# Fewer history tiles fetched by address on SyncE, and two TensorE layers replaced by ScalarE operations, in an attention kernel for recommendation

## The chip, the cores and the metric

The kernel runs on one core of a Trainium2 chip. The time is device microseconds of one execution; the number before is the median of three runs.

The engines are written as the profile writes them: PE is TensorE, DVE is VectorE, ACT is ScalarE, POOL is GpSimd and SP is SyncE. POOL, ACT and SP can also issue DMA transfers.

## What is computed

A batch of 16384 users has 200 history positions each. For each position the item's row of 64 floats is looked up in a table of 100000 rows, weighed by a small attention network, and summed:

```python
h = i_emb[hist]                                  # (200, 16384, 64)
itb = jnp.broadcast_to(it[None], h.shape)
feat = jnp.concatenate([h, itb, h - itb, h * itb], axis=-1)
a = dice(feat @ au_W1 + au_b1, au_alpha, axis=1)  # 36 units
w = a @ au_W2 + au_b2
cur = jnp.sum(w * jax.lax.stop_gradient(h), axis=0)
z = jnp.concatenate([u, it, c, cur], axis=-1)
z = dice(z @ W1 + b1, alpha1, axis=0)
z = dice(z @ W2 + b2, alpha2, axis=0)
return z @ W3 + b3
```

with

```python
def dice(x, alpha, axis):
    mean = jnp.mean(x, axis=axis, keepdims=True)
    var = jnp.var(x, axis=axis, keepdims=True)
    p = jax.nn.sigmoid((x - mean) * jax.lax.rsqrt(var + EPS))
    return x * (p + alpha * (1.0 - p))
```

The statistics of `dice` in the attention run over the whole batch, so the gate of position l can be made only when all of position l has gone through the first layer.

## The kernel before

A *tile* is 128 table rows of 64 floats. A history position l has 128 tiles, worked on in ND = 8 *chunks* of TD = 16 tiles. A step `step(k)` stands for one chunk, k = 8 l + c. Positions 0 to 179 run in a hardware loop of two passes of LPB = 90 positions, and the last 20 stand outside of it, before the head. The order of instructions on each engine is the order in which the program is written.

**How rows arrive.** Two ways are used.

- `fetch(k)` has POOL gather tiles: one indirect DMA for each tile of 128 rows (line 124), into `rows[k % 5]`, with indices from `idx`.
- The last tile of the chunks in SIDES = (3, 5, 7), three tiles of each l, comes *by address*. The 384 indices of l are loaded (`load_addresses`, line 137), scaled to byte offsets on DVE at step c = 4 of the position before (`scale_addresses`, line 141), read into registers, and each row is fetched by one small DMA of its own (`ask`, line 294) into one of BUFS = 6 buffers `side`. SPLIT = 0.5 gives half of each step's share, 24 rows, to SP and half to ACT. The wait for a tile's 128 rows and the copy into `rows` are DVE's (`place_tile`, line 392).

So NC = 125 tiles of each l are gathered by POOL and 3 come by address.

**What a step does.** In the order of the program, step k:

1. POOL: the gathers of chunk k.
2. ACT: `hidden(k-2)` moves the first layer's sums out of PSUM, `px` to `xs` (line 377). At the end of a position DVE makes its mean and variance (`moments`).
3. SP and ACT: the rows by address of this step. ACT's part stands partly before and partly behind the gate.
4. ACT: `gate(k-9)` makes the sigmoid from `xs` into PSUM `pg` (line 366).
5. DVE: `place(k-1)` copies the side tile if there is one; `turn(k-1)` transposes `rows` into `hT` by four instructions (line 149).
6. PE, still in `turn`: a layer with the identity matrix `unit` copies `hT` into PSUM `ph`; two layers with `blk_h` and `blk_i` add to `px`.
7. DVE: the statistics of chunk k-2 (line 382); `product(k-1)` multiplies `ph` by the item's rows into `hm` (line 412), and PE adds the layer with `blk_m` to `px`.
8. DVE: `weights(k-9)` multiplies gate and `xs` into `y` (line 369). PE adds `blk_x` times `xs` and `blk_p` times `y` in `wb`: `blk_x` carries alpha times the second layer's weights, `blk_p` carries one minus alpha times them, so their sum is the second attention layer behind `dice`.
9. DVE: `weigh(k-9)` multiplies `wb` by `hT` (line 373) and adds it to `curT` (line 374).

All layers have one helper, line 154; in the trace one layer of a chunk is four matmul instructions of 128x512.

The user rows are gathered in the same way in the last eight steps, with the tiles of chunks 3 and 5 by address; the item rows are gathered in the set-up, with no tile by address.

Of the kernel before, what the change touches and what calls it, by code (L numbers as in the profile page):

```python
# [11 lines left out]
AF = mybir.ActivationFunctionType  # L12
ALU = mybir.AluOpType
PSUM = bass.MemoryType.PSUM

P = 128
# [7 lines left out]
LAG = 9  # L24
XR = 8
IDX = 3
SIDES = (3, 5, 7)
BUFS = 6
LOAD = 28
SPLIT = 0.5  # L30
ROW = 4 * D
U8 = mybir.dt.uint8

# [2 lines left out]
def din_kernel(  # L36
# [24 lines left out]
    nc = tc.nc  # L61
# [8 lines left out]
    ZB = Z1 - ZA  # L70
    NS = len(SIDES)
    serial = iter(range(10**6))
# [8 lines left out]
    def make(name, *shape, dt=F32):  # L81
        return const.tile(list(shape), dt, name=name)

    def col(v):
        return v.rearrange("(p o) -> p o", o=1)

    def quarter(e, g, n=S):
        return slice((2 * e + g) * S, (2 * e + g) * S + n)


    def column(c, n):
        if c in SIDES and n == TD - 1:
            return NC + SIDES.index(c)
        return c * TD + n - sum(s < c for s in SIDES)

# [4 lines left out]
    ph = psum.tile([P, CD], F32, name="ph")  # L100
    pg = psum.tile([P, CD], F32, name="pg")
    wb = psum.tile([P, CD], F32, name="wb")

    rows = [make(f"rows{i}", P, TD, D) for i in range(ROWS)]
    hT = [make(f"hT{i}", P, CD) for i in range(LAG)]
    xs = [make(f"xs{i}", P, CD) for i in range(XR)]
# [3 lines left out]
    y = make("y", P, CD)  # L110
# [35 lines left out]
    def transpose(dst, of, n=slice(0, TD)):  # L146
        for i in range(2):
            for e in range(2):
                nc.vector.transpose(by_tile(dst[ts(e, D)], i)[:, n], of[ts(i, D), n, ts(e, S)])  # L149

    def layer(dst, pairs, first=True, last=True):
        for i in range(2):
            for j, (lhsT, rhs) in enumerate(pairs):
                nc.tensor.matmul(  # L154
                    dst[:, ts(i, CH)], lhsT, rhs[:, ts(i, CH)],
                    start=(first and j == 0), stop=(last and j == len(pairs) - 1),
                    skip_group_check=not (first and last),
                )
# [24 lines left out]
    blk_i = make("blk_i", P, P)  # L183
    blk_m = make("blk_m", P, P)
    blk_p = make("blk_p", P, P)
    blk_x = make("blk_x", P, P)
    unit = make("unit", P, P)
    au_w = make("au_w", P, 4, A)
    au_bias = make("au_bias", P, 1)
    au_al = make("au_al", P, 1)  # L190
    au_1al = make("au_1al", P, 1)
# [4 lines left out]
    def attention_weights():  # L196
        for t in (blk_h, blk_i, blk_m, blk_p, au_bias, au_al, au_w2):
            nc.vector.memset(t, 0.0)
        nc.sync.dma_start(au_bias2, au_b2.partition_broadcast(P))
        for e in range(2):  # L200
            w = au_W1.rearrange("(g d) a -> d g a", d=D)[e * S : (e + 1) * S]
            for g in range(2):
                r = quarter(e, g)
                nc.sync.dma_start(au_w[r], w)
                for q, (a0, n) in enumerate(halves):
                    c, a = quarter(q, g, n), slice(a0, a0 + n)
                    nc.vector.tensor_add(blk_h[r, c], au_w[r, 0, a], au_w[r, 2, a])
                    nc.vector.tensor_sub(blk_i[r, c], au_w[r, 1, a], au_w[r, 2, a])
                    nc.vector.tensor_copy(blk_m[r, c], au_w[r, 3, a])
                    nc.vector.memset(blk_p[r, quarter(q, g)], 1.0)  # L210
        for g in range(2):
            for q, (a0, n) in enumerate(halves):
                r, a = quarter(q, g, n), slice(a0, a0 + n)
                nc.sync.dma_start(au_bias[r], col(au_b1)[a])
                nc.sync.dma_start(au_al[r], col(au_alpha)[a])
                nc.sync.dma_start(au_w2[r], au_W2[a])
        nc.vector.tensor_scalar(au_1al, au_al, -1.0, 1.0, ALU.mult, ALU.add)
        nc.vector.tensor_mul(au_1al, au_1al, au_w2)
        nc.vector.tensor_mul(au_al, au_al, au_w2)
        nc.vector.tensor_scalar_mul(blk_x, blk_p, au_al)  # L220
        nc.vector.tensor_scalar_mul(blk_p, blk_p, au_1al)
        nc.vector.tensor_copy(unit, lanes)
        nc.vector.tensor_single_scalar(unit, unit, float(P), ALU.is_equal)


    w1a = make("w1a", P, 4, P)
# [13 lines left out]
    lanes, lane = (ucT[i][:, :P].bitcast(I32) for i in range(2))  # L240
# [40 lines left out]
    def tiles_by_address(l):  # L281

        return l * NS, range(NS)
# [20 lines left out]
    def shares(n, s, split):  # L304

        many = round(n * split)
        runs = []
        for r0, end in ((s * n, s * n + many), (s * n + many, (s + 1) * n)):
            loads = -(-(end - r0) // LOAD)
            at = [r0 + (end - r0) * i // loads for i in range(loads + 1)]  # L310
            runs.append(list(zip(at, at[1:])))
        return runs

    def ask(queue, runs, first, tiles, at, table):
        engine = queues[queue][0]
        flat = table.rearrange("v d -> (v d)").bitcast(U8)

        def place_of(r):
            return tiles[r // P] * P + r % P

        for r0, end in runs:
            while r0 < end:
                many = end - r0
                while place_of(r0 + many - 1) != place_of(r0) + many - 1:
                    many -= 1
                _, loaded = nc.values_load_multi_w_load_instructions(
                    at[:, place_of(r0) : place_of(r0) + many],
                    engines=(engine,), min_val=0, max_val=ROW * (table.shape[0] - 1),
                    skip_runtime_bounds_check_because="scale_addresses holds the address to the table",
                )  # L330
                for r, a in enumerate(loaded, r0):
                    m, p = first + r // P, r % P
                    key = keys.setdefault(m, f"rows{next(serial)}")
                    dma = row_by_address(
                        queue,
                        side[m % BUFS].bitcast(U8)[p : p + 1],
                        flat[ds(a, ROW)].rearrange("(o d) -> o d", o=1),
                    ).then_inc(landed[m % BUFS], 16)
                    tc.no_tile_sem_insts.add(dma.ins.name)
                    tc.add_to_no_dep_group(key, dma.ins)  # L340
                r0 += many

    def ask_hist(k, queue, some):
        l, s = divmod(k, ND)
        first, tiles = tiles_by_address(l)
        runs = shares(len(tiles) * P // ND, s, SPLIT)[queue]
        ask(queue, runs[some], first, tiles, addr[l % 3], i_emb)
# [7 lines left out]
    def has_side(k):  # L355
        return k % ND in SIDES

# [6 lines left out]
    def gate(k):  # L364
        i = k // ND % 3
        nc.scalar.activation(pg, xs[k % XR], AF.Sigmoid, bias=shifts[i], scale=rstds[i])  # L366

    def weights(k):
        nc.vector.tensor_mul(y, pg, xs[k % XR])  # L369
        layer(wb, [(blk_x, xs[k % XR]), (blk_p, y)])  # L370

    def weigh(k):
        nc.vector.scalar_tensor_tensor(wb, wb, au_bias2, hT[k % LAG], ALU.add, ALU.mult)  # L373
# [10 lines left out]
    def place(k):  # L384
        if has_side(k):
            l, c = divmod(k, ND)
            first, tiles = tiles_by_address(l)
            place_tile(k, first + tiles.index(SIDES.index(c)))

    def place_tile(k, m):  # L390
        await_rows(m)
        nc.vector.tensor_copy(rows[k % ROWS][:, TD - 1], side[m % BUFS])  # L392
# [12 lines left out]

    def turn(k):
        transpose(hT[k % LAG], rows[k % ROWS])
        layer(ph, [(unit, hT[k % LAG])])
        layer(px, [(blk_h, hT[k % LAG]), (blk_i, itT[k % ND])], last=False)

    def product(k):
# [23 lines left out]
    def step(k, last=None, weighed=()):  # L435

        def has(j):
            return last is None or j <= last

        ends = (k - 2) % ND == ND - 1  # L440
        if has(k):
            fetch(k)
        if has(k - 2):
            hidden(k - 2)
            if ends:
                measure(k - 2)
                moments((k - 2) // ND)
        if has(k):
            ask_hist(k, 0, slice(None))
            ask_hist(k, 1, slice(0, 1))  # L450
        if k - LAG not in weighed:
            gate(k - LAG)
        if has(k):
            ask_hist(k, 1, slice(1, None))
        if has(k - 1):
            place(k - 1)
            turn(k - 1)
        if has(k - 2) and not ends:
            measure(k - 2)
        if has(k - 1):  # L460
            product(k - 1)
        if k - LAG not in weighed:
            weights(k - LAG)
            weigh(k - LAG)
# [336 lines left out]
```

## Time and profile before

| | us |
|---|---|
| median of three runs | 31699.99 |
| the three runs | 31647.45, 31703.36, 31699.99 |
| the profiled execution | 31646.96 |
| its span, first to last instruction | 31645.1 |
| PE busy | 20823.3 (66%) |
| DVE busy | 15548.7 (49%) |
| ACT busy | 3817.4 (12%) |
| POOL busy | 23853.6 (75%) |

The mean granted TensorE clock was 0.806. The rows of the profile that follow below are read so: a group of instructions is given by line, engine, operation, output and inputs, shapes and count; then its busy time in us and the mean of one in ns; then the idle time of the engine just before them, with what ended most of it. "issue" marks idle time in which the engine waited for nothing that the profile shows.

### The profile page before, as it was taken

How to read it: one execution, taken by the hardware profiler on the slowest of the kernel's cores; microseconds unless marked ns; L12 is line 12 of the kernel's file. 1: busy time of each engine (PE TensorE's matmuls, PEld its weight loads, DVE VectorE, ACT ScalarE, POOL GpSimd, SP SyncE). 2: the span in 40 equal slices, each digit the busy share in tenths (PEclk: the TensorE clock that was granted, in tenths of full speed). 3: DMA queues.
4: the chain of work that ended last, by engine and by line, in shares of the span. 5: the costliest groups of instructions: out<-in, count | busy, mean ns of one | idle time of the engine just before them, and what ended most of it. 6: DMA issues, size and time to landing. Idle time of an engine off the chain costs nothing.

```text
span 31645.1 us, 223489 instructions
## 1 busy us (share of the span) xinstructions
PE 20823.3 (66%) x39536; PEld 8584.9 (27%) x39536; DVE 15548.7 (49%) x21275; ACT 3817.4 (12%) x3322; POOL 23853.6 (75%) x25259
## 2 busy tenths in 40 slices
PE   6666666666666666666666666666666666666666
PEld 2222222222222222222222222222222222222222
DVE  5444444444444444444444444444444444444445
ACT  1111111111111111111111111111111111111111
POOL 7777777777777777777777777777777777777776
PEclk8888788887888888888788888887878788887888
DMA  2111111111111111111111111111111111111111
GB/s 44 28 28 28 28 28 28 28 28 28 28 28 28 28 28 28 28 28 28 28 28 28 28 28 28 28 28 28 28 28 28 28 28 28 28 28 28 28 28 30
DMA packets 1008142, 894.16 MB, mean 28 GB/s; under 512 B 597358, under 2 KB 597559, under 8 KB 1006695
## 3 DMA queue, kind: packets, MB, share of 16 engines
q0 software_dynamic: 808128, 829.14, 15.0%
q1 hardware_dynamic: 114362, 27.92, 0.4%
q10 hardware_dynamic: 84205, 22.70, 0.3%
q14 instruction: 1136, 9.31, 0.1%
q8 instruction: 311, 5.10, 0.1%
HBM read 873.48 MB, written 4.39 MB: 28 GB/s over the span
## 4 chain that ended last, share of the span: by engine, by line
POOL 30%; issue 11%; PE 6%; DMA 5%; DVE 2%; DVEq 0%; ACT 0%; POOLq 0%; ACTq 0%
POOL rows L124 30%; DMA rows<-in_L_rec_i_emb,idx 5%; PE px L154 3%; PE ph L154 2%; PE wb L154 2%; DVE hT L149 1%; DVE wb L373 1%; DVE curT L374 0%; DVE st L382 0%; DVEq L149 0%; DVE mv L418 0%; DVE rows L392 0%; DVE addrs L141 0%; POOLq L124 0%; PE pg L154 0%
## 5 line engine op out<-in xcount | busy, mean ns | idle before, releaser
L124 POOL DMA_INDIRECT rows<-in_L_rec_i_emb,idx x25000 | 23591.6, 944 | 7633.1 <-issue 7166.6
L154 PE MATMUL ph<-hT,unit 128*128 128x512 f32 x6404 | 5969.6, 1088 | 10697.5 <-DVE hT L149 10697.5
L373 DVE SCALAR_TENSOR_TENSOR wb<-wb,au_bias,hT 128x1024 f32<-128x1024 f32 x1609 | 2079.7, 1293 | 10748.4 <-PE wb L154 10748.4
L149 DVE STREAM_TRANSPOSE hT<-rows 64x512 f32<-64x512 f32 x6404 | 4518.5, 706 | 2971.8 <-DMA rows<-in_L_rec_i_emb,idx 2529.3
L154 PEld LDWEIGHTS ph<-hT,unit 128*128 128x128 f32 x6404 | 1796.1, 311 | 13756.3 <-DVE hT L149 13561.4
L154 PE MATMUL px<-hT,blk_h 128*128 128x512 f32 x6404 | 4065.3, 723 | 0.0
L377 ACT ACTIVATE xs<-px,au_bias 128x1024 f32<-128x1024 f32 x1602 | 1784.1, 1114 | 14492.6 <-PE wb L154 14492.5
L366 ACT ACTIVATE pg<-xs,sh,rs 128x1024 f32<-128x1024 f32 x1609 | 1943.3, 1208 | 12967.9 <-issue 10092.6
L154 PE MATMUL px<-itT,blk_i 128*128 128x512 f32 x6404 | 3382.0, 610 | 0.0
L154 PE MATMUL wb<-y,blk_p 128*128 128x512 f32 x6436 | 3291.1, 593 | 11.3 <-DVE y L369 11.3
L154 PE MATMUL wb<-xs,blk_x 128*128 128x512 f32 x6436 | 3289.2, 593 | 2.6 <-DVE curT L374 2.6
L154 PE MATMUL px<-hm,blk_m 128*128 128x512 f32 x6408 | 3011.3, 592 | 0.0
L412 DVE TENSOR_TENSOR hm<-ph,itT 128x1024 f32<-128x1024 f32 x1601 | 1960.4, 1224 | 1934.9 <-PE ph L154 1934.9
L154 PEld LDWEIGHTS px<-hT,blk_h 128*128 128x128 f32 x6404 | 1627.8, 254 | 2406.1 <-issue 2304.8
L382 DVE BATCH_NORM_STATS2 st<-xs 128x6 f32<-128x512 f32 x3204 | 2058.4, 684 | 44.5 <-ACT pg L366 0.3
L369 DVE TENSOR_TENSOR y<-pg,xs 128x1024 f32<-128x1024 f32 x1609 | 1955.7, 1215 | 85.0 <-ACT pg L366 82.9
L374 DVE TENSOR_TENSOR curT<-wb,curT 128x1024 f32<-128x1024 f32 x1609 | 1969.8, 1224 | 54.8
L154 PEld LDWEIGHTS px<-itT,blk_i 128*128 128x128 f32 x6404 | 1404.8, 219 | 2000.0 <-issue 2000.0
L154 PEld LDWEIGHTS wb<-y,blk_p 128*128 128x128 f32 x6436 | 1224.5, 190 | 1551.8 <-issue 1537.2
L154 PEld LDWEIGHTS wb<-xs,blk_x 128*128 128x128 f32 x6436 | 1224.3, 190 | 1541.4 <-issue 1538.0
L154 PEld LDWEIGHTS px<-hm,blk_m 128*128 128x128 f32 x6408 | 1219.0, 190 | 1531.4 <-issue 1524.2
L124 POOL DMA_INDIRECT rows<-in_L_rec_i_emb,ids x125 | 139.7, 1118 | 39.6 <-issue 37.2
(180 smaller groups left out, 1779.3 us busy)
## 6 DMA issues: line engine op xcount, KB each, us to landing
side<-in_L_rec_i_emb SPq DMA_DIRECT2D x38400, 0.2 KB
side<-in_L_rec_i_emb ACTq DMA_DIRECT2D x38400, 0.2 KB
rows<-in_L_rec_i_emb,idx POOLq DMA_INDIRECT x25000, 2.5
idx<-in_r_hist SPq DMA_DIRECT2D x200, 62.5 KB
hT<-cs ACTq DMA_DIRECT2D x16, 500.0 KB
ucT<-catT SPq DMA_DIRECT2D x8, 512.0 KB
side<-in_L_rec_u_emb SPq DMA_DIRECT2D x256, 0.2 KB
addrs<-in_r_hist SPq DMA_DIRECT2D x200, 1.5 KB
```

The costliest lines, as they stand in the source:

```text
L124: nc.gpsimd.indirect_dma_start(out=dst[:, n, :], out_offset=None, in_=table, in_offset=bass.IndirectOffsetOnAxis(ap=ids, axis=0),)
L149: nc.vector.transpose(by_tile(dst[ts(e, D)], i)[:, n], of[ts(i, D), n, ts(e, S)])
L154: nc.tensor.matmul(dst[:, ts(i, CH)], lhsT, rhs[:, ts(i, CH)], start=(first and j == 0), stop=(last and j == len(pairs) - 1), skip_group_c ...
L366: nc.scalar.activation(pg, xs[k % XR], AF.Sigmoid, bias=shifts[i], scale=rstds[i])
L369: nc.vector.tensor_mul(y, pg, xs[k % XR])
L373: nc.vector.scalar_tensor_tensor(wb, wb, au_bias2, hT[k % LAG], ALU.add, ALU.mult)
L374: nc.vector.tensor_add(curT[k % ND], wb, curT[k % ND])
L377: nc.scalar.activation(xs[k % XR], px, AF.Identity, bias=au_bias)
L382: nc.vector.bn_stats(stats[l % 3][:, 2 * c + i, :], xs[k % XR][:, ts(i, CH)])
L412: nc.vector.tensor_mul(hm, ph, itT[k % ND])
```

## The change

Three constants and four places in the code change.

- SIDES goes from (3, 5, 7) to (7,): one tile of each l, 128 rows, comes by address, and 127 are gathered by POOL. NC, the number of columns of `idx` and the number of addresses follow from it. The user pass, which takes the tiles of chunks 3 and 5 by address where they are in SIDES, then has none by address.
- SPLIT goes from 0.5 to 1.0: all rows by address are issued by SP, 16 in each step, and ACT issues none in the steps.
- In `turn`, a copy on ACT from `hT` to `ph` takes the place of the layer with `unit`.
- In `gate`, a second activation on ACT makes `au_1al` times the sigmoid plus `au_al`, in place in PSUM; `weights` then multiplies by `xs` on DVE as before, and PE has the one layer `blk_p` (of ones) instead of `blk_x` and `blk_p`. The matrices `unit` and `blk_x` and their making fall away.

```diff
-SIDES = (3, 5, 7)
+SIDES = (7,)
...
-SPLIT = 0.5
+SPLIT = 1.0
...
-        nc.vector.tensor_scalar_mul(blk_x, blk_p, au_al)
-        nc.vector.tensor_scalar_mul(blk_p, blk_p, au_1al)
-        nc.vector.tensor_copy(unit, lanes)
-        nc.vector.tensor_single_scalar(unit, unit, float(P), ALU.is_equal)
...
-            loads = -(-(end - r0) // LOAD)
+            loads = max(1, -(-(end - r0) // LOAD))
...
     def gate(k):
         i = k // ND % 3
         nc.scalar.activation(pg, xs[k % XR], AF.Sigmoid, bias=shifts[i], scale=rstds[i])
+        nc.scalar.activation(pg, pg, AF.Identity, bias=au_al, scale=au_1al)

     def weights(k):
         nc.vector.tensor_mul(y, pg, xs[k % XR])
-        layer(wb, [(blk_x, xs[k % XR]), (blk_p, y)])
+        layer(wb, [(blk_p, y)])
...
     def turn(k):
         transpose(hT[k % LAG], rows[k % ROWS])
-        layer(ph, [(unit, hT[k % LAG])])
+        nc.scalar.copy(ph, hT[k % LAG])
         layer(px, [(blk_h, hT[k % LAG]), (blk_i, itT[k % ND])], last=False)
```

More of the change, by code (lines that the diff above doesn't have):

```diff
@@ L185, in din_kernel @@
     blk_p = make("blk_p", P, P)
-    blk_x = make("blk_x", P, P)
-    unit = make("unit", P, P)
     au_w = make("au_w", P, 4, A)
```

## The prediction

> **What bounds the kernel now.** I read the page first: the busy shares, then the chain that ended last.
>
> ```profile
> span 31645.1 us, 223489 instructions
> PE 20823.3 (66%) x39536; PEld 8584.9 (27%) x39536; DVE 15548.7 (49%) x21275; ACT 3817.4 (12%) x3322; POOL 23853.6 (75%) x25259
> POOL 30%; issue 11%; PE 6%; DMA 5%; DVE 2%; DVEq 0%; ACT 0%; POOLq 0%; ACTq 0%
> ```
>
> No engine is busy all the time, and the chain accounts for 54% of the span only: it names a suspect, POOL and the "issue" gaps between its instructions, and proves nothing. So I read next all that POOL does, the gathers into `rows`, with what its idle time waited for (columns of the first rows: shortest/median/longest in ns, then the first and last start in us; of the others: us in total, times).
>
> ```profile
> L124 POOL DMA_INDIRECT rows<-in_L_rec_i_emb,idx x25000: 940/944/1120, 184.6 to 31408.0; - x199
> L124 POOL DMA_INDIRECT rows<-in_L_rec_i_emb,ids x125: 940/953/11142, 2.9 to 182.1; - x125
> L124 POOL DMA_INDIRECT rows<-in_L_rec_u_emb,ids x125: 940/944/961, 31409.2 to 31564.1; - x125
> L124 POOL DMA_INDIRECT rows<-in_L_rec_u_emb,side_ids x1: 944/944/944, 31565.3 to 31565.3; - x1
> ...
>   issue: 7241.2, 23739
>   DMA rows<-in_L_rec_i_emb,idx: 336.0, 1102
>   DVE rows L392: 55.2, 157
> ```
>
> The 25000 history gathers start evenly over 31223.4 us, so one starts every 31223.4 / 24999 = 1.249 us: 0.944 us of work and a gap. The gap put down to "issue" is 7241.2 / 23739 = 0.305 us, and the one put down to another gather 336.0 / 1102 = 0.305 us: the same, so neither is a wait for data. POOL therefore issues gather after gather without a stall that counts, from 184.6 us to 31565.3 us; 79.8 us of head follow, and before it stand 184.6 us. The number of gathers sets the time.
>
> Next, whether anything else is near that pace. The waits of DVE, which works on each chunk of 16 tiles (1600 chunks):
>
> ```profile
> DVE wb L373 <- PE wb L154: 10748.4, 1609, 7.5
> DVE hT L149 <- DMA rows<-in_L_rec_i_emb,idx: 2529.3, 1181, 5.0
> DVE hm L412 <- PE ph L154: 1934.9, 1601, 2.4
> ```
>
> The second row is the important one: DVE runs out of gathered rows, 2529.3 / 1600 = 1.6 us in each chunk. The consumers wait for POOL; they follow it closely, but they follow.
>
> **The change part by part.** *The gathers.* With SIDES = (7,) each history position l has 127 tiles of 128 by gather instead of 125. Over 200 positions that is 400 more instructions on POOL, and in the user pass at the end, where tiles 3 and 5 came by address, 2 more (128 for 126); the item pass keeps its 128. Each costs the pace above, on the engine that sets the end: 402 x 1.249 = 502.1 us. The gather of 128 rows is the same instruction on the same tables, so the price is not in doubt by more than the pace may shift; see the rivals.
>
> *The rows by address.* They go from 384 to 128 per l, all on SP:
>
> ```profile
> side<-in_L_rec_i_emb SPq DMA_DIRECT2D x38400, 0.2 KB
> side<-in_L_rec_i_emb ACTq DMA_DIRECT2D x38400, 0.2 KB
> SPq L326 <- DVE rows L392: 15047.6, 198, 84.3
> 15000.00 12.24 SPq L294 DMA_DIRECT2D side<-in_L_rec_i_emb  x36
> ```
>
> SP issues 192 per l now and ACT 192; after, SP issues 128 and ACT none. At 12.24 / 36 = 0.34 us each, a step's 16 rows take SP 5.4 us of about 19.8. SP also waits 15047.6 us (76 us per l) for a side buffer to be emptied, which means that it runs far ahead. With one tile per l the six buffers reach six positions back, so that wait goes, and SP waits instead for the next l's addresses, which DVE scales at step 4 of the l before. The last 16 rows of an l are thus asked for long before the step that places them. Cost on the path: 0. If that cover were gone, the placing copy on DVE would stand up to 5.4 us once per l, with the transposes behind it; POOL would feel it only beyond the five `rows` buffers. Bounds: 0 to 200 x 5.4 = 1080 us; I take 0.
>
> *TensorE's two layers that go, and ScalarE's two operations that come.* Rows of the costliest groups (busy us, mean ns of one, idle before):
>
> ```profile
> L154 PE MATMUL ph<-hT,unit 128*128 128x512 f32 x6404 | 5969.6, 1088 | 10697.5 <-DVE hT L149 10697.5
> L154 PE MATMUL wb<-xs,blk_x 128*128 128x512 f32 x6436 | 3289.2, 593 | 2.6 <-DVE curT L374 2.6
> L377 ACT ACTIVATE xs<-px,au_bias 128x1024 f32<-128x1024 f32 x1602 | 1784.1, 1114 | 14492.6 <-PE wb L154 14492.5
> L366 ACT ACTIVATE pg<-xs,sh,rs 128x1024 f32<-128x1024 f32 x1609 | 1943.3, 1208 | 12967.9 <-issue 10092.6
> L149 DVE STREAM_TRANSPOSE hT<-rows 64x512 f32<-64x512 f32 x6404 | 4518.5, 706 | 2971.8 <-DMA rows<-in_L_rec_i_emb,idx 2529.3
> L382 DVE BATCH_NORM_STATS2 st<-xs 128x6 f32<-128x512 f32 x3204 | 2058.4, 684 | 44.5 <-ACT pg L366 0.3
> L373 DVE SCALAR_TENSOR_TENSOR wb<-wb,au_bias,hT 128x1024 f32<-128x1024 f32 x1609 | 2079.7, 1293 | 10748.4 <-PE wb L154 10748.4
> L374 DVE TENSOR_TENSOR curT<-wb,curT 128x1024 f32<-128x1024 f32 x1609 | 1969.8, 1224 | 54.8
> L412 DVE TENSOR_TENSOR hm<-ph,itT 128x1024 f32<-128x1024 f32 x1601 | 1960.4, 1224 | 1934.9 <-PE ph L154 1934.9
> L369 DVE TENSOR_TENSOR y<-pg,xs 128x1024 f32<-128x1024 f32 x1609 | 1955.7, 1215 | 85.0 <-ACT pg L366 82.9
> ```
>
> Per chunk PE loses 5969.6 / 1601 + 3289.2 / 1609 = 5.8 us. ACT gains two activations of 128x1024. A copy from SBUF to PSUM and an Identity from PSUM to PSUM are not in the loop today; the nearest rows are 1.114 us (PSUM to SBUF) and 1.208 us (SBUF to PSUM), and I take the dearer: 2.4 us per chunk. ACT then works 1.114 + 1.208 + 2.4 = 4.7 us of a step of 15.875 x 1.249 = 19.8 us. Sigmoid and Identity already alternate, and the program loads no more tables than before.
>
> Where it lies: `hm` on DVE must now wait for ACT's copy instead of PE's four matmuls, 1.1 to 1.2 us after the last transpose; the statistics that DVE runs meanwhile take 2 x 0.68 us of it, so that wait shrinks rather than grows. The copy waits for the transposes, and behind it on ACT's queue stands only the next step's `hidden`, which needs this very chunk's `px` anyway. The gate no longer queues behind ACT's own row DMAs (the idle of 10092.6 us under "issue", 8 us each time), so its second activation is done before `y` needs it. All of it lies behind the gathers: cost 0. As a bound: even if all 16 remaining matmuls ran at the pace of the slow first four (5969.6 / 6404 = 0.93 us each), a step on DVE would be two transposes 1.4 + PE 14.9 + `weigh` 1.29 + 1.22 = 18.8 us, plus the per-l statistics, which are DVE's 15548.7 / 1600 = 9.7 us a chunk less 9.1 us for the six kinds of the rows above (their busy times add to 14542 us over 1600 chunks), so 0.6: 19.4 us, still under 19.8. If the consumers did pass POOL's pace, each us over it would cost 1600 us. From the other side, faster consumers gain nothing, since POOL waits for none of them.
>
> *Set-up and head.* Four small DVE operations and a few small DMAs less at the start, a few activations more in the user pass: a few us either way, taken as 0 with bounds of -10 and +10.
>
> **The sum.** The profiled execution took 31646.96 us, 1.9 us more than its span. 31646.96 + 502.1 = 32149 us. The three timed runs lie at 31647.45, 31699.99 and 31703.36: two values 53 to 56 us apart, of which the profiled execution shows the lower. On the median, 31699.99, the sum is 32202. Nothing in the profile says which of the two the changed kernel will show, so I forecast the middle, 32175 us, 1.5 to 1.6% slower.
>
> **The rivals.**
>
> *Faster: the rows by address slow the gathers down.* 51200 of them go from the history passes. If each held up POOL by 502.1 / 51200 = 9.8 ns, the change would come out even; at twice that it gives 31647 - 502 = 31145 us. For it speaks only that both end in the same DMA engines. Against it speaks the user pass, of which one stretch (31409 to 31459 us) has row DMAs and a later one (31509 to 31559) has none:
>
> ```profile
> side<-in_L_rec_u_emb SPq DMA_DIRECT2D x35, 0.2 KB
> ...
> L124 POOL DMA_INDIRECT rows<-in_L_rec_u_emb,ids x40 | 37.8, 944 | 12.2 <-issue 11.3 <-DMA rows<-in_L_rec_u_emb,ids 0.6 <-DVE mv L418 0.3
> ...
> L124 POOL DMA_INDIRECT rows<-in_L_rec_u_emb,ids x40 | 37.8, 944 | 12.2 <-issue 11.9 <-DMA rows<-in_L_rec_u_emb,ids 0.3
> ```
>
> Forty gathers of 944 ns and 12.2 us of gaps in both: the rows cost POOL nothing. Chance 2%.
>
> *Less slow: the placing copies hold POOL up.* DVE copies each side tile into `rows`, and 400 of these copies go:
>
> ```profile
> L392 DVE COPY rows<-side 128x64 f32<-128x64 f32 x603 | 128.1, 212 | 12.0 <-PEq L580 4.9 <-DMA rows<-in_L_rec_i_emb,idx 3.0
> ```
>
> If POOL stood for the whole of each, 400 x 0.212 = 85 us come back: 32149 - 85 = 32064 us, or 32117 on the median. Against it: the longest history gather is 1120 ns, and the 157 gaps that end on this copy average 55.2 / 157 = 0.35 us, over the usual gap by 7 us in all. Chance 4%. The Trainium skill, page "SBUF — State Buffer", section "SBUF: two separate sides", would have it so: an fp32 copy within SBUF takes the port pair that VectorE shares with GpSimd, and GpSimd cannot write its DMA descriptors until the copy ends. By that rule the 85 us are gained; the gap of 0.35 us here shows next to none of it.
>
> *Slower still: the single tile comes late, or the step on DVE passes 19.8 us.* The first costs up to 1080 us: 32149 + 1080 = 33229; the second 1600 us for each us over, so 33749 at one. For it: the last rows are asked for only one step ahead in program order, and a chain of PE and ACT hand-overs remains. Against it: SP's 76 us per l of waiting, and DVE's 1.6 us of slack per chunk, to which the shorter PE work adds. Chance 4%. That the change does not do what it says would need fewer gathers than counted; the loop in `fetch` leaves no room for it.
>
> **How the numbers follow.** Forecast 90%, the three rivals 2, 4 and 4%. The forecast's own values, 32149 and 32202, with 10 us of set-up on either side and up to 50 us for a run as far above its neighbours as the timed ones are from each other, give 32090 to 32270; the bounds of 85 us below and 1080 us above are left to the rivals outside, under 2 in 10 together. Against 0.2% (63 us), which is what two measurements of this kernel can tell apart: slower 0.97, faster 0.02, within 0.01.
>
> **What would show it.** Right: 25400 history gathers at 0.944 us with gaps of 0.305, starting every 1.249 us; the first near 185 us, the last user gather near 32068 and the end 80 us later; PE busy lower by some 9250 us, ACT higher by some 3900; DVE waiting longer for gathered rows than 2529 us. Wrong: a pace under 1.23 us (faster), gaps on POOL that end on DVE's transposes or copies (consumers too slow), or DVE standing before the copy in `place_tile` for side rows.

## The result, and the profile after

| | before | changed |
|---|---|---|
| median, us | 31699.9 | 32190.34 |
| runs, us | 31647.45 to 31703.36 | 32147.96 to 32196.47 |
| the profiled execution, us | 31646.96 | 32147.96 |

The changed kernel takes 1.0152 of the time before, 95% interval 1.014 to 1.0164: 490 us more by the medians, 501 us more by the profiled executions. On two other chips, where the three versions that ran there took 20 to 32% longer than here, the order was the reverse; that is told in the last section, and all that stands before it, but for the last table of the experiments and two lines beside it, is from chips where the kernel before takes 31647 to 31703 us.

The page of the changed kernel, with the same lines as were shown of before (PEld is the loading of weights for PE):

```profile
span 32146.2 us, 148139 instructions
PE 15240.8 (47%) x26696; PEld 6209.0 (19%) x26696; DVE 15316.0 (48%) x20869; ACT 7186.4 (22%) x6532; POOL 24231.4 (75%) x25661
POOL 6%; issue 2%; DMA 1%; PE 1%; DVE 1%; ACT 0%; DVEq 0%; POOLq 0%
```

PE has lost a quarter of its work, ACT has nearly doubled its own, POOL is busy for the same 75% of a longer span. The chain now covers about 11% of the span, less still than before, so it is of no more use here. What POOL did (shortest/median/longest in ns, first and last start in us; then idle time by releaser):

```profile
L124 POOL DMA_INDIRECT rows<-in_L_rec_i_emb,idx x25400: 938/944/992, 186.4 to 31907.2; - x199
L124 POOL DMA_INDIRECT rows<-in_L_rec_u_emb,side_ids x1: 947/947/947, 32066.9 to 32066.9; - x1
...
  issue: 7415.1, 24325
  DMA rows<-in_L_rec_i_emb,idx: 342.0, 1122
```

25400 gathers, one each (31907.2 - 186.4) / 25399 = 1.249 us, with the gap of 7415.1 / 24325 = 0.305 us. The pace is what it was; there are 400 more of them. The waits of the engines that use the rows:

```profile
ACT ph L403 <- DVE hT L149: 14295.3, 1599, 11.4
DVE hT L149 <- DMA rows<-in_L_rec_i_emb,idx: 8449.9, 1497, 7.6
DVE wb L368 <- PE wb L154: 7256.1, 1609, 5.5
DVE hm L407 <- ACT ph L403: 221.5, 202, 2.6
```

DVE now waits 8449.9 us for gathered rows where it waited 2529.3, and less for PE and for `ph`. DVE gets through the rest of its step sooner, although ACT has more work than before, and what it saves turns into waiting for POOL.

### The profile page after: what moved, and what is told of

It reads as the page before. It is cut to its first block, busy times and chain, and to the rows that moved or that the text cites. A ratio compares the mean times of both kernels' runs of the same rounds, so it can differ in the third digit from the quotient of the medians.

```text
span 32146.2 us, 148139 instructions
## 1 busy us (share of the span) xinstructions
PE 15240.8 (47%) x26696; PEld 6209.0 (19%) x26696; DVE 15316.0 (48%) x20869; ACT 7186.4 (22%) x6532; POOL 24231.4 (75%) x25661
## 5 line engine op out<-in xcount | busy, mean ns | idle before, releaser
L124 POOL DMA_INDIRECT rows<-in_L_rec_i_emb,idx x25400 | 23965.8, 944 | 7756.3 <-issue 7340.1
L154 PE MATMUL px<-hT,blk_h 128*128 128x512 f32 x6404 | 5665.9, 983 | 16766.8 <-DVE hT L149 16314.4
L149 DVE STREAM_TRANSPOSE hT<-rows 64x512 f32<-64x512 f32 x6404 | 4520.4, 706 | 8959.7 <-DMA rows<-in_L_rec_i_emb,idx 8449.9
L154 PEld LDWEIGHTS px<-hT,blk_h 128*128 128x128 f32 x6404 | 1815.2, 314 | 19641.0 <-issue 16971.4
L403 ACT COPY ph<-hT 128x1024 f32<-128x1024 f32 x1601 | 1627.1, 1016 | 14295.3 <-DVE hT L149 14295.3
L154 PE MATMUL px<-itT,blk_i 128*128 128x512 f32 x6404 | 4733.1, 832 | 0.0
L154 PE MATMUL wb<-y,blk_p 128*128 128x512 f32 x6436 | 3028.3, 593 | 16.6 <-DVE y L364 16.6
L154 PEld LDWEIGHTS px<-itT,blk_i 128*128 128x128 f32 x6404 | 1860.5, 291 | 2863.6 <-issue 2863.6
L407 DVE TENSOR_TENSOR hm<-ph,itT 128x1024 f32<-128x1024 f32 x1601 | 1935.1, 1209 | 221.5 <-ACT ph L403 221.5
L361 ACT ACTIVATE pg<-pg,au_al,au_1al 128x1024 f32<-128x1024 f32 x1609 | 1893.8, 1177 | 53.5
L417 DVE COPY other<-mv 32x2 f32<-32x2 f32 x804 | 150.0, 187 | 15.0
L124 POOL DMA_INDIRECT rows<-in_L_rec_u_emb,ids x127 | 119.8, 944 | 38.7 <-issue 36.6
```

The source lines that it names most:

```text
L124: nc.gpsimd.indirect_dma_start(out=dst[:, n, :], out_offset=None, in_=table, in_offset=bass.IndirectOffsetOnAxis(ap=ids, axis=0),)
L154: nc.tensor.matmul(dst[:, ts(i, CH)], lhsT, rhs[:, ts(i, CH)], start=(first and j == 0), stop=(last and j == len(pairs) - 1), skip_group_c ...
L361: nc.scalar.activation(pg, pg, AF.Identity, bias=au_al, scale=au_1al)
L403: nc.scalar.copy(ph, hT[k % LAG])
L407: nc.vector.tensor_mul(hm, ph, itT[k % ND])
```

## The experiments

Each row of a table below compares with runs of the kernel before on the same chip.

**One part alone, and the suspected cost taken away.** The first kernel is the kernel before with the constants of the change alone (there are two, not three, SIDES and SPLIT; the third line, the `max`, only keeps a share of no rows from dividing by zero):

```diff
-SIDES = (3, 5, 7)
+SIDES = (7,)
-SPLIT = 0.5
+SPLIT = 1.0
-            loads = -(-(end - r0) // LOAD)
+            loads = max(1, -(-(end - r0) // LOAD))
```

> One tile by address, on SP, with the computation of the kernel before. Theory (gathers alone): 402 more gathers at 1.249 us, so 502 us over the kernel before, 32149 us (32202 for runs of the upper value), the same as the changed kernel within 20 us. Rival (the computation on ScalarE has a share in the loss): clearly under 32149, by whatever that share is. DVE's wait for gathered rows then grows only by the slower pace, from 1.6 to about 1.9 us per chunk.

The second is the changed kernel with the old constants, so with ScalarE's copy and linear part alone:

```diff
-SIDES = (7,)
+SIDES = (3, 5, 7)
-SPLIT = 1.0
+SPLIT = 0.5
```

> Three tiles by address on both queues as before, with the copy and the gate's linear part on ScalarE. Theory: the gathers are 25000 as before, so 31647 us (31700), unchanged within 20 us, with a pace of 1.249 us; TensorE's busy time falls by about 5600 us for nothing. Rival (consumers too slow): the copy stands on ScalarE's queue behind some 24 row DMAs of 7.3 us and two activations of the gate, a step passes 19.5 us, and each us over it costs 1600 us, so 33000 or more, with gaps on POOL that end on DVE's transposes.

The third is the changed kernel that leaves the gathers of two tiles of each l out, so that old rows stand in their place:

```diff
-        for n in range(TD - has_side(k)):
+        for n in range(TD - (c in (3, 5, 7))):
```

> The changed kernel without the gathers of the last tiles of chunks 3 and 5 (left out of the computation's input: those rows of the buffers keep what an earlier chunk left there). Theory: 400 gathers less at 1.249 us, 499.6 us under the changed kernel, 31648 us (31697). Rival (what costs is not the gathers but the row DMAs' placing or ScalarE's part): stays at 32148.

| kernel | median, us | before there, us | ratio, 95% interval |
|---|---|---|---|
| constants alone | 32155.87 | 31661.8 | 1.0155 (1.0138 to 1.0172) |
| ScalarE's part alone | 31658.53 | 31661.8 | 0.9999 (0.999 to 1.0009) |
| changed, two gathers of each l left out | 31653.54 | 31661.8 | 0.9997 (0.9988 to 1.0007) |

The constants alone cost 494 us and ScalarE's part costs nothing. Without the 400 gathers the changed kernel is back at the time before. The gathers are the whole of the loss. The gathers of the kernel with the constants alone:

```profile
L124 POOL DMA_INDIRECT rows<-in_L_rec_i_emb,idx x25400: 940/945/992, 185.3 to 31919.8; - x199
```

and those of the kernel with ScalarE's part alone:

```profile
L124 POOL DMA_INDIRECT rows<-in_L_rec_i_emb,idx x25000: 940/945/1125, 184.6 to 31417.5; - x199
```

With 128 rows by address per l the pace is (31919.8 - 185.3) / 25399 = 1.2494 us, with 384 it is (31417.5 - 184.6) / 24999 = 1.2494 us: the row DMAs of one or of three tiles take nothing from POOL.

**The other way: more tiles by address.** The kernel before with one constant changed, three times:

```diff
-SIDES = (3, 5, 7)
+SIDES = (1, 3, 5, 7)
```

> The kernel before with four tiles by address, SIDES = (1, 3, 5, 7). Theory: the price of a gather holds on this side too, 200 gathers less, 249.8 us under the kernel before, 31397 us (31450). Rival (queues or consumers give out): each queue issues 32 rows in a step of 19.4 us, some 10 us; if that delays the gate or the placing by over DVE's slack of 1.6 us per chunk, the step grows and the time stays at 31650 or goes above it.

```diff
-SIDES = (3, 5, 7)
+SIDES = (1, 3, 4, 6, 7)
```

> The kernel before with five tiles by address, SIDES = (1, 3, 4, 6, 7). Theory: 400 gathers less than with three, one more in the user pass (chunk 5 has no tile by address there), 498 us under the kernel before, 31163 us on a chip where that takes 31662. Rival (consumers give out): each queue issues 40 rows in a step, ACT 12.2 us; if DVE's slack of 1.4 us per chunk with four tiles is used up, the time stays at four tiles' 31418 or goes above.

```diff
-SIDES = (3, 5, 7)
+SIDES = (1, 2, 3, 5, 6, 7)
```

> The kernel before with six tiles by address, SIDES = (1, 2, 3, 5, 6, 7). Theory: 600 gathers less, 748 us under the kernel before, 30914 us. Rival: SP needs some 16 us and ACT 14.7 + 2.3 us of a step of 19.05 us, and late rows or a late gate make the step longer; then gaps on POOL that end on DVE, and a time above five tiles'.

And the changed kernel with six tiles on both queues:

```diff
-SIDES = (7,)
+SIDES = (1, 2, 3, 5, 6, 7)
-SPLIT = 1.0
+SPLIT = 0.5
```

> Six tiles by address on both queues with the copy and the gate's linear part on ScalarE. Theory: ACT has 14.7 us of rows and 4.5 us of its own in a step of 19.05 us, 19.2 us, so it just becomes the bound or nearly so: 30914 to 31400 us, above six tiles with TensorE's layers. Rival (the place of the work between ACT and PE does not matter at any number of tiles): the same as six tiles within 20 us.

| tiles by address | median, us | before there, us | ratio, 95% interval |
|---|---|---|---|
| four | 31418.42 | 31661.8 | 0.9923 (0.9907 to 0.994) |
| five | 31161.48 | 31649.21 | 0.9846 (0.9829 to 0.9862) |
| six | 33058.8 | 31649.21 | 1.0442 (1.0425 to 1.0459) |
| six, ScalarE's part | 41959.39 | 31649.21 | 1.3257 (1.3235 to 1.3279) |

Four and five tiles gain 243 and 488 us, 1.2 us for each gather that goes (200, and 400 less one more in the user pass), and five tiles is the fastest version found: 1.5% under the kernel before and 3.0% under the changed one by the ratios of the two. At six the price turns over. POOL's waits, and DVE's for side rows, with six tiles:

```profile
POOL rows L124 <- issue: 6248.6, 19646, 3.9
POOL rows L124 <- DMA rows<-in_L_rec_i_emb,idx: 3305.5, 4877, 3.2
DVE rows L392 <- DMA side<-in_L_rec_i_emb: 2087.4, 321, 14.5
```

The second row is the new one: 4877 gaps of 0.68 us on average, over twice the usual 0.305, that end when an earlier gather has landed. Beyond the usual gap they hold 3305.5 - 4877 x 0.305 = 1818 us, most of the 2145 us by which the kernel misses the forecast of 30914. The time from issue to landing says why. Its shortest, median and longest with five tiles:

```profile
DMA to landing us min/median/max: 2.3/3.1/15.5
```

and with six:

```profile
DMA to landing us min/median/max: 2.3/8.8/14.0
```

Each gather waits for the one eight before it: the gathers use eight semaphores in turn, and where the trace names the gather whose landing ended a gap of over 0.4 us, it is the eighth before in 3584 of 3596. Eight gathers of 1.249 us are 10 us. The longest landings say nothing (15.5 us with five tiles, more than with six); how many pass 10 us does. Of the 3040 history gathers of the six-tile trace whose landing can be told, 32% land later than 10 us, and with five tiles none of 6131. So the gathers and the row DMAs do get in each other's way: the landing lengthens a little at 640 rows per l (a median of 3.1 us for 2.5 before), and the pace breaks at 768. It is not the number alone, since the next kernel asks for 768 rows as well, in longer steps, and there the median is 2.5 us; where the two meet stays open. By the third row side tiles come late too, but gaps that end on DVE make up only some 70 us on POOL. The rival's outcome came true, a time above that of five tiles, and not by its mechanism (gaps on POOL that end on DVE); the slow landing of the gathers was in neither theory.

With ScalarE's part at six tiles the limit is elsewhere. One step of that kernel, in order of time, on ACT and what hangs on it:

```profile
15005.47 1.21 ACT L360 ACTIVATE pg<-xs,sh,rs 128x1024 f32<-128x1024 f32 x1 [8.22 <-DVE st L377]
15006.71 1.18 ACT L361 ACTIVATE pg<-pg,au_al,au_1al 128x1024 f32<-128x1024 f32 x1
15008.45 7.82 ACTq L288 DMA_DIRECT2D side<-in_L_rec_i_emb  x24
15016.31 1.02 ACT L403 COPY ph<-hT 128x1024 f32<-128x1024 f32 x1 [8.43 <-issue]
15017.36 1.22 DVE L407 TENSOR_TENSOR hm<-ph,itT 128x1024 f32<-128x1024 f32 x1 [11.93 <-ACT ph L403]
...
15022.45 1.11 ACT L372 ACTIVATE xs<-px,au_bias 128x1024 f32<-128x1024 f32 x1 [5.13 <-PE px L154]
15024.20 7.44 ACTq L288 DMA_DIRECT2D side<-in_L_rec_i_emb  x24
```

The copy needs ACT's queue, `hm` needs the copy, `px` needs `hm`, the next `hidden` needs `px`, and on ACT's queue two lots of 24 row DMAs, 7.8 and 7.4 us, stand between `hidden` and the next copy. The loop is closed through ACT, and POOL now waits for DVE's transposes (11124.3 us), so a step takes 41959 / 1600 = 26 us. My expectation had added up ACT's work (19.2 us) and set it against POOL's step, and missed that the row DMAs lie in series with the chain. With three tiles the same arrangement costs nothing, as the second kernel of the first group shows.

**Copies on DVE.** Does a copy within SBUF stop POOL? The changed kernel with eight more copies in each step, of the shape of the placing copy:

```diff
+    spare = make("spare", P, D)
...
+        for _ in range(8):
+            nc.vector.tensor_copy(spare, itT[0][:, :D])
         if has(k - 1):
             product(k - 1)
```

> The changed kernel with eight more copies of 128x64 on DVE in every step, of the shape of the placing copy, 12800 or so in all. Theory (the copies do not hold POOL up): DVE has over 5 us of slack in a step and takes 1.7 us more, so the pace stays 1.249 us and the time within 30 us of the changed kernel's, 32150 to 32190. Rival (POOL stands still for the whole of a copy): 12800 x 0.212 = 2714 us more, 34860, with gathers of up to 1.15 us.

One execution took 32199.46 us. Its copies, and its gathers:

```profile
L457 DVE COPY spare<-itT 128x64 f32<-128x64 f32 x12872 | 2900.4, 225 | 392.0
```

```profile
L125 POOL DMA_INDIRECT rows<-in_L_rec_i_emb,idx x25400: 939/947/1005, 185.1 to 31958.8; - x199
```

2900 us of copies lie in the trace and the execution is 51 us longer than the profiled changed kernel, but only 3 to 15 us longer than the other three executions of that kernel; the longest gather is 1005 ns, less than 944 + 225. The gathers of this trace can be sorted by what ran beside them: 21287 had no copy beside them and last 945.5 ns in the mean, and 1641 had more than 0.6 us of copies beside them and last 945.7 ns. A copy does not stop a gather.

The 51 us are found in the gathers. POOL's busy time in them in the changed kernel, and in the one with the copies:

```profile
L124 POOL DMA_INDIRECT rows<-in_L_rec_i_emb,idx x25400 | 23965.8, 944 | 7756.3 <-issue 7340.1
L125 POOL DMA_INDIRECT rows<-in_L_rec_i_emb,idx x25400 | 24016.1, 946 | 7758.8 <-issue 7343.1
```

That is 50.3 us, 2 ns in each gather, with a copy beside it or without. Whether they come with the copies was asked by more runs, the kernel with the copies twice and the two kernels to compare it with:

> The changed kernel with eight more copies in every step once more, beside the changed kernel itself on the same chip. Theory (the 51 us of the first look over the profiled changed kernel are the upper of the two values that every version shows, with a gather of 947 instead of 944 ns): equal to the changed kernel within 15 us when runs of the same gather time are compared. Rival (each copy costs POOL some 4 ns): 51 us above it in every run.

> The changed kernel, for the run beside it: 32148 to 32160 us, or some 50 us more where its gathers take 947 ns.

> The kernel before, for a trace of it beside the next run. Theory where gathers set the pace: 31647 to 31664 us, a gather of 944 or 945 ns, or some 50 us more where it is 947. Where the chip is such that the times stand at 38700 to 41800 us as in the last pair: gaps on POOL that end on DVE, and DVE, ACT and SP standing still together for 5 us and more with nothing that the trace names.

> The changed kernel with eight more copies in every step, against the kernel before. Theory (copies do not hold POOL up): 502 us over the kernel before, ratio 1.0159, as for the changed kernel, within 15 us where the gather time is the same. Rival (some 4 ns a copy): 553 us over, ratio 1.0175. Where the pair's times stand at 39000 us, no answer.

All of these runs fell on the chips where everything is slower, so their times give no answer:

| kernel | median, us | before there, us | ratio, 95% interval |
|---|---|---|---|
| changed, extra copies | 39305.26 | 41797.0 | 0.9401 (0.9385 to 0.9416) |
| changed | 38769.19 | 41797.0 | 0.9278 (0.9262 to 0.9293) |
| before | 41750.06 | 41729.01 | 1.0005 (0.9995 to 1.0014) |
| changed, extra copies | 39399.54 | 41729.01 | 0.9444 (0.9428 to 0.946) |

Their traces do. The gathers of the changed kernel, without the copies, and then of the first kernel with them:

```profile
L124 POOL DMA_INDIRECT rows<-in_L_rec_i_emb,idx x25400: 941/947/1412, 252.7 to 38409.1; - x199
L125 POOL DMA_INDIRECT rows<-in_L_rec_i_emb,idx x25400: 938/944/1413, 252.2 to 39022.9; - x199
```

Here the longer gather, 947 ns, stands in the kernel without the copies and the shorter in the one with them; the second kernel with the copies shows 944 as well. So the 51 us are not the price of the copies, but the upper of two values that the next section comes back to.

## Why the prediction was right, step by step

*The gathers set the time.* Right, and shown: by the constants alone (494 us more), by leaving 400 gathers out (back to the time before) and by the gain of four and five tiles. The sum of the profiled execution, 32149 us, met 32147.96; the last user gather was put at 32068 us and started at 32066.9, and 79.3 us of head followed. That the two meet within about 1 us is luck in one respect: both profiled executions show the lower of the two values that the next paragraph is about.

*The middle of two values.* The runs of the changed kernel lie at 32147.96 and at 32184.93 to 32196.47, 37 to 49 us apart, so that its median lies among the upper ones. No execution took the 32175 us of the forecast: the middle was a hedge, and that the median came within 15 us of it is luck. A trace of the upper value was not at hand for the prediction. The kernel with five tiles gives one: its profiled execution took 31219.4 us, its other three 31157.44 to 31163.25, and in that trace

```profile
L124 POOL DMA_INDIRECT rows<-in_L_rec_i_emb,idx x24600: 940/947/1255, 186.2 to 30977.3; - x199
```

the median gather takes 947 ns instead of 944 or 945. POOL's busy time in the gathers, with five tiles and then in the kernel before:

```profile
L124 POOL DMA_INDIRECT rows<-in_L_rec_i_emb,idx x24600 | 23270.6, 946 | 7521.8 <-issue 7218.1
L124 POOL DMA_INDIRECT rows<-in_L_rec_i_emb,idx x25000 | 23591.6, 944 | 7633.1 <-issue 7166.6
```

That is 23270.6 / 24600 = 0.9460 us for a gather and 23591.6 / 25000 = 0.9437: 2.3 ns in 24600 gathers are 57 us, of the 56 to 62. The 51 us of the execution with the extra copies are of the same kind. In these traces the two values are a matter of the gather's own length, through the whole execution; the upper executions of the kernel before and of the changed kernel were not traced, and what sets the length stays open. There are more than two values: on the chip of the first group of experiments all 19 executions of the kernel before took 31658 to 31664 us, and gathers of 945 ns stand in all traces from there.

*SP's rows cost nothing.* Right. SP's longest wait has moved from the side buffers to the addresses, as was said:

```profile
SPq L320 <- DVE addrs L141: 14325.4, 197, 109.2
```

*ScalarE's two operations lie behind the gathers.* Right, shown by ScalarE's part alone at 0.9999. The prices were bounded by 1.114 and 1.208 us and the dearer taken for both; the rows say

```profile
L403 ACT COPY ph<-hT 128x1024 f32<-128x1024 f32 x1601 | 1627.1, 1016 | 14295.3 <-DVE hT L149 14295.3
L361 ACT ACTIVATE pg<-pg,au_al,au_1al 128x1024 f32<-128x1024 f32 x1609 | 1893.8, 1177 | 53.5
```

The copy is cheaper than either bound, 1.016 us. The bound from below was too high, and ACT's busy time rose by 7186.4 - 3817.4 = 3369 us instead of some 3900; it had no effect, since the work is hidden. The wait of `hm` shrank, from 1934.9 to 221.5 us, as was said.

*TensorE loses 9250 us.* Wrong in size: it lost 20823.3 - 15240.8 = 5582 us. The removed layer was the first of each step and had the slow matmuls; the layers that now come first have them instead:

```profile
L154 PE MATMUL px<-hT,blk_h 128*128 128x512 f32 x6404 | 5665.9, 983 | 16766.8 <-DVE hT L149 16314.4
L154 PE MATMUL px<-itT,blk_i 128*128 128x512 f32 x6404 | 4733.1, 832 | 0.0
```

Before they took 723 and 610 ns each:

```profile
L154 PE MATMUL px<-hT,blk_h 128*128 128x512 f32 x6404 | 4065.3, 723 | 0.0
L154 PE MATMUL px<-itT,blk_i 128*128 128x512 f32 x6404 | 3382.0, 610 | 0.0
```

In both kernels the slow matmuls stand first behind the long idle time and not in a certain layer, so taking the first layer away does not take them away. The mean granted clock fell from 0.806 to 0.718 with it; it is 0.721 with ScalarE's part alone and 0.799 with the constants alone. None of this reached the end time.

*The rivals.* That row DMAs slow the pace of the gathers is false at one, three, four and five tiles and true at six, where the gathers land late; it did not apply to this change. That placing copies hold POOL up is refuted by the 12872 extra copies. With them goes, for this kernel, what the prediction cites from the Trainium skill, page "SBUF — State Buffer", section "SBUF: two separate sides": by it most of the copies' 2900 us would have come on top, and in that trace the gathers with copies beside them are 0.2 ns longer than those without. The gathers that overlap a placing copy in the trace of before are 3 us longer in all than as many others, not 85. That the consumers pass POOL's pace does not happen with one tile; with six tiles and ScalarE's part it does.

## What to carry to other kernels

Where one engine issues without a stall that counts, a change is worth the number of its instructions times their pace, and all that is saved elsewhere turns into waiting for it; the first thing to compare in the trace of after is therefore that engine's count and pace. The two halves of this change were aimed in opposite directions, and only the half on the bound counted; the other half would have been the place to look if DVE's wait for rows had been gone. Work that is free on a queue at one load (24 row DMAs) is not free at twice the load when it stands in series with a chain that passes through the same queue.

## What was not expected of the hardware

*Two chips on which the kernels run 20 to 32% longer, in the opposite order.* Before takes 41729 to 41797 us there and the changed kernel 38769, a ratio of 0.9278. POOL's gathers in the trace of the changed kernel take what they take elsewhere, but POOL is stopped by DVE, and DVE and ACT stand for up to 35 us at a time before work whose inputs the profile does not name ("remote"):

```profile
DVE wb L368 <- remote: 16289.9, 696, 35.5
ACT xs L372 <- remote: 10143.9, 425, 27.3
POOL rows L124 <- issue: 7556.2, 24460, 9.8
POOL rows L124 <- DVE hT L149: 6307.2, 589, 23.7
```

In one such stretch SP needs 20.32 us for 15 row DMAs, where 32 take 10.64 us in the trace of the changed kernel from elsewhere (the first line below); the activations and DVE's operations last as long as elsewhere:

```profile
15017.65 10.64 SPq L288 DMA_DIRECT2D side<-in_L_rec_i_emb  x32
...
15000.45 20.32 SPq L288 DMA_DIRECT2D side<-in_L_rec_i_emb  x15
...
15015.93 1.29 DVE L368 SCALAR_TENSOR_TENSOR wb<-wb,au_bias,hT 128x1024 f32<-128x1024 f32 x1 [13.69 <-remote]
```

The extra time goes with the number of instructions in the trace, whatever the version:

| kernel | instructions | span there, us | span elsewhere, us | extra per instruction |
|---|---|---|---|---|
| before | 223489 | 41747.6 | 31645.1 | 45.2 ns |
| changed | 148139 | 38755.1 | 32146.2 | 44.6 ns |
| changed, extra copies | 161011 | 39376.2 | 32197.7 | 44.6 ns |

The last two rows come close to a test of it: on one chip the 12872 extra copies, which cost nothing elsewhere, make the profiled execution 621 us longer and the median 536, which is 42 to 48 ns for each instruction more. Each copy also brings 225 ns of work on DVE, which POOL waits for there, so the number of instructions did not change alone. All this points to the delivery of instructions to the engines, of which the changed kernel needs a third fewer (rows by address and matmuls that are gone), but it is argued and not shown, and what differs about these chips stays open. If it holds, the sign of the change is that of the gathers where POOL is the bound, and that of the instruction count there.
